# Two graph layers and two top-2 mixtures of experts: the choice of experts made panel by panel inside the convolutions, gates carried in the gathered rows, w3 resident instead of w1, second products two blocks behind

## The chip, the cores and the metric

The kernel runs on one core of a Trainium2 chip. TensorE (PE) multiplies, VectorE (DVE), ScalarE (ACT) and GpSimd (POOL) work element by element, and SyncE (SP) only issues transfers. Each engine takes its own instructions strictly in order and waits on semaphores for the others. The metric is the device time in microseconds of one execution, as the median over runs.

## The reference

There are N = 3125 nodes with 256 features (D) and 50000 edges (src, dst). Four residual blocks follow each other, each on the layernorm of x:

```python
def sage(x, W_l, b_l, W_r):                       # mean over incoming edges
    return (segment_sum(x[src], dst) / max(deg, 1)) @ W_l + b_l + x @ W_r

# block 1: two SAGE convolutions and a product
h = relu(sage(ln(x), W1_l, b1, W1_r)); h = relu(sage(h, W2_l, b2, W2_r))
x = x + h @ W3 + b3
# block 2: 16 experts of width 512, the best two of each node
p = softmax(ln(x) @ gate_w + gate_b); top2, renormalised to sum 1
x = x + sum_e gate_e * ((silu(ln(x) @ w1[e]) * (ln(x) @ w2[e])) @ w3[e])
# block 3: on ln(x): three GCN convolutions of the first 64 features (relu),
#          a dynamic convolution weighted by gelu(x @ W1 + b1) @ W2 + b2,
#          joined with the other 192 features
x = x + x_full @ W_aggr + b_aggr
# block 4: 8 experts of width 512, the best two, without gates
x = x + sum_e mask_e * (gelu(ln(x) @ W1[e] + b1[e]) @ W2[e] + b2[e])
```

## The kernel before

Nodes are held in NT = 25 tiles of 128 rows, grouped in panels of 512 (TPP = 4 tiles): six full ones and one of a single tile. A dense matrix of edge counts is built once in fp8 (`at8`) and both graph layers multiply with it. The program is written in the order of the computation. A framework assigns the tiles to memory pools, sets the semaphores, and orders each engine's instructions ahead of the run by their place in the program and by modelled times; at run time each engine keeps that order. A tile with `bufs=k` may have k instances alive, and a new one waits until the oldest is no longer read.

**Convolutions of layer 0.** `sage` walks the panels. For each, `panel_of` casts 25 blocks of `at8` into `blk` tiles (128x512), five alive at once. `cast` shares them out by their number over ACT and DVE, and over POOL too in the second graph (where `three` is set and seven tiles are alive). PE multiplies each block into `pa` (line 576), the sums are copied to `agg` (582), and then every tile gets its products and its `done` function. For conv2 this is `convolution2`: when a panel is done, it stores x to `xb0`, normalises into `rows` (lines 384 to 390; the square root is ACT's), stores these to `xnd0` by SP, transposes each tile and writes its scores into the kept tile `scores0` (516).

**Choice of experts.** It starts when all panels are done, behind an If (line 718) whose body is for graphs that cannot take the fast way. `resident` loads the whole of w1 (16 loads of 512 KB, line 865) on ACT's queue. Then softmax over all 25 tiles at once (lines 970 to 975), `top2` (400 elements per operation), and `route`: PE forms the running counts of each expert in f32, and every chosen pair of node and expert gets a position in a list sorted by expert, in blocks of 128 rows. To invert that list, `route` runs a loop over two choices of 25 tiles each: DVE makes a one-hot `row` (835) and a two-part `what` (837, 845) of node number and gate, and PE multiplies them (848). The result is `idx`, the node of every row of every block, and `gate` (855, 857).

**Experts.** `experts` walks the blocks, 64 in layer 0 and 56 in layer 1. `begin` issues the block's streamed weights on SP and the gather of its rows on POOL (897), two blocks ahead. `hidden` transposes the rows (`pt`, `xT`), multiplies with the first weights (`ph`, 918) and forms `hid`. `finish`, one block behind, transposes `hid`, multiplies with the last weight (`pe`, 937 and 942), scales with the gate into `y` (944), and POOL adds `y` to `xb` by an indirect DMA (945). In layer 0 w1 is resident and w2 and w3 are streamed, 1 MB per block; in layer 1 both weights are resident, and a broadcast bias of 256 KB is streamed.

**Second graph.** The rows are read back and normalised. Three GCN passes walk the panels (`pc`, line 1096), and with the first two go the dynamic convolution's panels. In the last pass `finish` makes the output rows of a panel: products, the residual sum, normalisation, transposes and scores into `scores1`. Then `resident` loads both weights of layer 1 on ACT's queue, and `top2`, `route` and `experts` run again.

Of the kernel before, what the change touches and what calls it, by code (L numbers as in the profile page):

```python
# [8 lines left out]
F32 = mybir.dt.float32  # L9
# [9 lines left out]
P = 128  # L19
N = 3125  # L20
# [32 lines left out]
def kernel(ctx: ExitStack, tc: tile.TileContext, a, out: bass.AP):  # L53
# [20 lines left out]
    def open_rows(c):  # L74
        here["rows"] = c.enter_context(tc.tile_pool(name="rows", bufs=2))
# [40 lines left out]
    scores0 = keep.tile([P, NT, NE0], F32, name="scores0")  # L116
    scores1 = keep.tile([P, NT, NE1], F32, name="scores1")
# [4 lines left out]
    xnd0, xnd1, xb0, xb1 = (dram.tile([NR, D], F32, name=n) for n in ("xnd0", "xnd1", "xb0", "xb1"))  # L122
# [10 lines left out]
    def build_sorted(c):  # L133
# [4 lines left out]
        sums = scores1.rearrange("p t e -> p (t e)")[:, : 2 * NG]  # L138
        gl = c.enter_context(tc.tile_pool(name="sl", bufs=1))
        gk = c.enter_context(tc.tile_pool(name="sk", bufs=2))  # L140
        gw = c.enter_context(tc.tile_pool(name="sw", bufs=3))
# [41 lines left out]
        def prepare():  # L183
            for i, (c0, w) in enumerate(PANELS):
# [41 lines left out]
                ohr = gk.tile([P, P, WN], F16, name="ohr", bufs=1)  # L226
# [24 lines left out]
        def count():  # L251
# [3 lines left out]
            for g in range(NG):  # L255
                w0 = g * GW
                ohk = gw.tile([P, 2, NF, 4], F16, name="ohk")
                onehot(ohk, io_key, keys[:, w0 : w0 + GW], 2)
                ohl = gw.tile([P, 2, P, 4], F16, name="ohl")
# [177 lines left out]
    def panel_of(exact, loads, c0, w, three=False):  # L437

        if not exact:
            for k in range(NT):  # L440
                blk = loads.tile([P, PW], F32R, name="blk", bufs=7 if three else 5)
                cast(k, blk[:, :w], at8[c0 // PW][:, k, :], three)
                yield k, blk[:, :w]
            return
# [38 lines left out]
    def top2(s, n, small):  # L483

        def first_max(v, i):
            m = small.tile([P, NT], F32, name=f"m{i}")
            nc.vector.tensor_reduce(m, v, AX.X, OP.max)
            hit = small.tile([P, NT, n], F32, name=f"hit{i}")  # L490
            nc.vector.tensor_tensor(hit, v, m[:, :, None].to_broadcast([P, NT, n]), OP.is_equal)
            nc.vector.scalar_tensor_tensor(
                hit, hit, -float(P), iota[:, None, :n].to_broadcast([P, NT, n]), op0=OP.mult, op1=OP.add
            )
            at_ = small.tile([P, NT], F32, name=f"at{i}")
            nc.vector.tensor_reduce(at_, hit, AX.X, OP.min)
            nc.vector.tensor_scalar(at_, at_, float(P), None, op0=OP.add)
            oh = small.tile([P, NT, n], F32, name=f"oh{i}")
            nc.vector.tensor_tensor(
                oh,  # L500
                iota[:, None, :n].to_broadcast([P, NT, n]),
                at_[:, :, None].to_broadcast([P, NT, n]),
                OP.is_equal,
            )
            return m, oh

        m1, oh1 = first_max(s, 1)
        rest = small.tile([P, NT, n], F32, name="rest")
        nc.vector.scalar_tensor_tensor(rest, oh1, -3e38, s, op0=OP.mult, op1=OP.add)
        m2, oh2 = first_max(rest, 2)  # L510
        return m1, oh1, m2, oh2

    def scores(s, xT, t, w, bias, n):
        pg = ps_one("pg", [P, n])
        product(pg, xT, w)
        nc.vector.tensor_add(s[:, t, :], pg, bias)


    class First:


        def __init__(self, c):
            self.pool = lambda name, bufs: c.enter_context(tc.tile_pool(name=name, bufs=bufs))
            self.rows = self.pool("rows0", NT + 1)
# [10 lines left out]
        def weights2(self, c):  # L535
            cw = c.enter_context(tc.tile_pool(name="cw2", bufs=1))
# [88 lines left out]
    def convolution2(f, exact, loads):  # L625
# [15 lines left out]
        for panel in sage(f, exact, loads, parts, f.w2l, f.b2, own[1], done2):  # L641
# [7 lines left out]
            nc.sync.dma_start(rows_in(xnd0, c0, w), rows[:, :n, :])  # L649
            for i in range(n):  # L650
                xT = f.n.tile([P, KD, P], F32, name="xT")
                transpose_tile(xT, rows[:, i, :])
                scores(scores0, xT, c0 // P + i, f.gw, f.gb, NE0)
# [8 lines left out]
    with ExitStack() as c:  # L662
# [45 lines left out]
        open_psum(ctx, 2)  # L708
        with ExitStack() as c1:
            open_rows(c1)  # L710
            behind = rows_tile()[:, 0, :]
            nc.vector.memset(behind, 0.0)
            for t in (xnd0, xnd1, xb0, xb1):
                nc.scalar.dma_start(t[NP:, :], behind)
# [492 lines left out]
```

## Time and profile before

| what | time |
|---|---|
| runs of the kernel | 1933.12 us median (1928.09 to 1934.69) |
| profiled execution | 1928.86 us, span 1927.1 us, clock 0.916 |
| end of conv2's scores to first expert transpose, layer 0 | 623.58 to 711.48 |
| experts of layer 0 | 712 to 1112 |
| second graph's passes | 1166 to 1560 |
| last scores to first expert transpose, layer 1 | 1560.17 to 1611.10 |
| experts of layer 1 | 1611 to 1909 |

Times are microseconds from the start of the span. The page's slices cut the span in 40 parts of about 48 us, and a digit is the busy share of an engine in tenths; PEclk is the granted clock of TensorE in the same scale. In a table of windows each row has the window, its sum, and per engine the busy time with the number of instructions. A row of the timeline gives start and duration, engine, line, the operation with its output and inputs, and in brackets how long the engine had been idle and what released it. A group row gives the busy time, the mean of one instruction in nanoseconds, and the idle time in front of the group. Names are the program's: `xg` are gathered rows, `xb` the rows to which results are added, `w_all` a resident weight.

### The profile page before, as it was taken

What the parts mean: (1) busy time and instruction counts of PE and PEld (TensorE: products, weight loads), DVE (VectorE), ACT (ScalarE), POOL (GpSimd) and SP (SyncE); (2) the same over time, 40 slices, a digit from 0 to 9 for tenths busy, and PEclk for the clock granted to TensorE, in tenths of its full rate; (3) what the DMA queues carried; (4) which work ended last, traced back from release to release, by engine and by line L of the source; (5) the groups of instructions that cost most, each with busy time, mean ns of one, the idle gap of its engine ahead of it and who ended that gap; (6) DMA issues with size and microseconds to landing.
All of it is one profiled execution on the core that took longest, in us unless ns stands there. A gap on an engine that the chain in (4) does not pass through costs nothing. (4 is left out here: it accounts for less than half of the span.)

```text
span 1927.1 us, 23952 instructions
## 1 busy us (share of the span) xinstructions
PE 1671.2 (87%) x7696; PEld 1159.7 (60%) x7696; DVE 879.0 (46%) x2298; ACT 660.8 (34%) x1574; POOL 492.2 (26%) x513
## 2 busy tenths in 40 slices
PE   5899999799997189999999937879889758999995
PEld 3777777677776055555555525546567545556553
DVE  5866664244542562222222266547547464333231
ACT  3766665233331002222222226437446101222221
POOL 4411110100000013444434334204213002544542
PEclk9999999899997559999999958999989757999998
DMA  3311111711210426777777630000002162444444
GB/s 115 104 53 47 47 48 36 243 45 44 66 48 29 175 93 193 216 217 213 212 211 213 174 96 18 1 1 1 1 8 92 58 218 54 104 102 99 101 102 103
DMA packets 145977, 192.81 MB, mean 100 GB/s; under 512 B 11728, under 2 KB 105279, under 8 KB 145775
## 3 DMA queue, kind: packets, MB, share of 16 engines
q1 hardware_dynamic: 106108, 137.28, 22.2%
q0 software_dynamic: 23936, 33.83, 9.7%
q10 hardware_dynamic: 15794, 20.01, 3.1%
q8 instruction: 68, 1.11, 0.2%
q14 instruction: 71, 0.57, 0.1%
HBM read 148.61 MB, written 45.67 MB: 101 GB/s over the span
## 5 line engine op out<-in xcount | busy, mean ns | idle before, releaser
L576 PE MATMUL pa<-blk,hl 128*128 128x512 f32 (+1 forms) x1400 | 366.0, 401 | 1.8 <-ACT blk L431 1.8
L897 POOL DMA_INDIRECT xg<-xnd,idx x120 | 118.1, 984 | 670.5 <-DVE gate L857 330.6
L576 PEld LDWEIGHTS pa<-blk,hl 128*128 128x128 f32 x1400 | 249.0, 196 | 43.5 <-ACT blk L431 2.3
L431 ACT CAST blk<-at 128x512 fp32r<-128x512 fp8e4 (+1 forms) x378 | 209.5, 572 | 125.7 <-PE pa L576 64.9
L918 PE MATMUL ph<-w_all,xT 128*128 x480 | 240.8, 625 | 9.5 <-ACT xT L399 0.4
L945 POOL DMA_INDIRECT xb<-y,idx x120 | 190.7, 1589 | 164.5 <-DMA xb<-y,idx 87.3
L433 DVE CAST blk<-at 128x512 fp32r<-128x512 fp8e4 (+1 forms) x392 | 171.7, 456 | 99.7 <-PE pa L576 75.9
L399 ACT COPY xT<-pt 128x256 f32<-128x256 f32 x195 | 72.6, 372 | 319.6 <-PE pt L398 317.8
L1096 PE MATMUL pc<-blk,g 128*128 128x512 f32 (+1 forms) x525 | 144.5, 411 | 16.3 <-ACT blk L431 12.9
L989 DVE TENSOR_TENSOR hid<-hid,ph 128x512 f32<-128x512 f32 x64 | 44.0, 687 | 239.7 <-ACT hid L988 239.7
L918 PEld LDWEIGHTS ph<-w_all,xT 128*128 128x128 f32 x480 | 80.4, 190 | 99.3 <-issue 62.2
L435 POOL CAST blk<-at 128x512 fp32r<-128x512 fp8e4 (+1 forms) x105 | 71.7, 689 | 256.6 <-PE pc L1096 172.9
L1096 PEld LDWEIGHTS pc<-blk,g 128*128 128x128 f32 x525 | 94.3, 200 | 49.4 <-issue 14.6
L937 PE MATMUL pe<-w,hTs 128*128 128x256 f32 x512 | 121.3, 379 | 1.0 <-ACT hTs L933 1.0
L937 PEld LDWEIGHTS pe<-w,hTs 128*128 128x128 f32 x512 | 97.0, 190 | 41.1 <-issue 29.7
L918 PE MATMUL ph<-w,xT 128*128 128x512 f32 x256 | 120.4, 592 | 0.0
L268 ACT ACTIVATE at<-pcount 128x400 fp8e4<-128x400 f32 x196 | 97.4, 502 | 49.4 <-PE pcount L264 48.2
L944 DVE TENSOR_SCALAR y<-pe,gate 128x256 f32<-128x256 f32 x120 | 58.1, 484 | 122.7 <-PE pe L942 94.1
L988 ACT ACTIVATE hid<-ph 128x512 f32<-128x512 f32 x64 | 38.2, 597 | 217.9 <-PE ph L918 217.9
L937 PE MATMUL pe<-w_all,hTs 128*128 x448 | 106.0, 379 | 1.8 <-ACT hTs L933 1.8
L937 PEld LDWEIGHTS pe<-w_all,hTs 128*128 128x128 f32 x448 | 85.0, 190 | 36.8 <-issue 25.8
L264 PE MATMUL pcount<-ohk,ohl 128*128 128x100 f16 x784 | 93.7, 271 | 3.0 <-ACT at L268 1.5
(251 smaller groups left out, 2358.1 us busy)
## 6 DMA issues: line engine op xcount, KB each, us to landing
w<-in_L_ffn_w_dram SPq DMA_DIRECT2D x128, 512.0 KB, 5.4
bin<-in_L_ffn_b_dram SPq DMA_DIRECT2D x56, 256.0 KB, 3.6
w_all<-in_L_ffn_w_dram ACTq DMA_DIRECT2D x16, 512.0 KB, 10.2
w_all<-in_L_ffn_W_dram ACTq DMA_DIRECT2D x16, 512.0 KB, 9.9
h1d<-hl SPq DMA_DIRECT2D x25, 256.0 KB, 2.0
hl<-h1d SPq DMA_DIRECT2D x25, 256.0 KB, 4.9
xp<-in_x_dram SPq DMA_DIRECT2D x12, 512.0 KB, 4.7
mine<-own SPq DMA_DIRECT2D x12, 512.0 KB, 3.9
```

The costliest lines, as they stand in the source:

```text
L264: nc.tensor.matmul(pw[:, w * NF : (w + 1) * NF], ohl[:, b, :, w], ohk[:, b, :, w], start=True, stop=True)
L268: nc.scalar.activation(at8[o // PW][:, :, o % PW : o % PW + 4 * WN].rearrange("p k (w r) -> p w k r", r=WN), pw[:, : 4 * NF].rearrange("p ...
L399: nc.scalar.copy(dst, pt)
L431: nc.scalar.copy(dst, src)
L433: nc.vector.tensor_copy(dst, src)
L435: nc.gpsimd.tensor_copy(dst, src)
L576: nc.tensor.matmul(pa[:, m, :w], parts[k][:, i, m * P : (m + 1) * P].bitcast(one), blk, start=(k == 0 and i == 0), stop=(k == NT - 1 and i ...
L897: nc.gpsimd.indirect_dma_start(out=xg, out_offset=None, in_=xnd[:, :], in_offset=bass.IndirectOffsetOnAxis(ap=idx[:, b : b + 1], axis=0),)
L918: ran.append(nc.tensor.matmul(ph[:, i, :], xT[:, k, :], weight_of(b, weights, i, k), start=(k == 0), stop=(k == KD - 1)))
L937: nc.tensor.matmul(po, hT[:, j, :], weight_of(b, weights, n_in, j), start=(j == 0), stop=(j == n_hid - 1 and b_out is None))
L945: nc.gpsimd.indirect_dma_start(out=xb[:, :], out_offset=bass.IndirectOffsetOnAxis(ap=idx[:, b : b + 1], axis=0), in_=y, in_offset=None, co ...
L1096: nc.tensor.matmul(pc[:, :w], g[:, k].rearrange("p i q -> p (i q)").bitcast(one), blk, start=(k == 0), stop=False,)
```

## The change

- A class `Router` takes the place of `top2` and of the first half of `route`. Its `panel` is called by conv2, and by `finish` of the second graph, once the scores of a panel stand. It makes the softmax (layer 0 only), the two best experts, gates, counts and ranks of the panel, with two f16 products on PE, and the one-hot rows of its tiles in f16, which stay in the kept tile `onehots`.
- Its `route` does what needs the totals: the first block of each expert, then for each of the two choices one comparison over all blocks and tiles at once, one product on DVE, one copy on ACT and 25 f16 products on PE.
- The gates of layer 0 and the numbers of their experts are written as four more columns of `xnd0`, one transfer per panel on SP. A gather brings them with the row, and `finish` picks the gate that belongs to the block's expert.
- w3 is the resident weight of layer 0, and w1 and w2 are streamed. The loads of `resident` go by POOL's queue instead of ACT's, in both layers.
- In layer 0 the second products run two blocks behind the first instead of one. `hid` gets three tiles, `xg` five; `y` has two instead of three in both layers.
- To make room: `blk` five tiles everywhere instead of seven in the second graph, `rows0` 25 tiles instead of 26, single instances of `rows`, `g`, `ew` and `nT` in the second graph, normalisation in place there. The constants are made before conv2.

The core of the diff (what is not shown: the build of the graph using `onehots` as scratch space, the way for other graphs, the constants):

```diff
-                blk = loads.tile([P, PW], F32R, name="blk", bufs=7 if three else 5)
+                blk = loads.tile([P, PW], F32R, name="blk", bufs=5)
...
+    class Router:
+        ohs_ = keep.tile([P, 2, NT, NE0], F16, name="ohs")
+        high = keep.tile([P, 2, NT], F32, name="high")
+        before_ = keep.tile([P, NT + 1, NE0], F16, name="before")
...
+        def panel(self, small, c0, s, gates=None):
...
+            if gates is not None:
+                red = tile_("red", [P, n])
+                nc.vector.tensor_reduce(red, s, AX.X, OP.max)
+                nc.vector.tensor_sub(s, s, wide(red))
+                nc.scalar.activation(s, s, AF.Exp)
+                nc.vector.tensor_reduce(red, s, AX.X, OP.add)
+                nc.vector.reciprocal(red, red)
+                nc.vector.tensor_mul(s, s, wide(red))
+            best, at_ = tile_("best", two), tile_("at", two)
+            v = s
+            for c in range(2):
+                nc.vector.tensor_reduce(best[:, c, :], v, AX.X, OP.max)
+                hit = tile_("hit")
+                nc.vector.tensor_tensor(hit, v, wide(best[:, c, :]), OP.is_equal)
+                nc.vector.scalar_tensor_tensor(
+                    hit, hit, -float(P), iota[:, None, :n_exp].to_broadcast(shape), op0=OP.mult, op1=OP.add
+                )
+                nc.vector.tensor_reduce(at_[:, c, :], hit, AX.X, OP.min)
+                nc.vector.tensor_scalar(at_[:, c, :], at_[:, c, :], float(P), None, op0=OP.add)
+                oh = self.ohs[:, c, t0 : t0 + n, :]
+                nc.vector.tensor_tensor(oh, iota[:, None, :n_exp].to_broadcast(shape), wide(at_[:, c, :]), OP.is_equal)
+                if c == 0:
+                    v = tile_("rest")
+                    nc.vector.scalar_tensor_tensor(v, oh, -3e38, s, op0=OP.mult, op1=OP.add)
+            if gates is not None:
+                nc.vector.tensor_add(red, best[:, 0, :], best[:, 1, :])
+                nc.vector.reciprocal(red, red)
+                for c in range(2):
+                    nc.vector.tensor_mul(gates[:, :n, c], best[:, c, :], red)
+                    nc.vector.tensor_copy(gates[:, :n, 2 + c], at_[:, c, :])
...
+            both = tile_("both", dtype=F16)
+            nc.vector.tensor_add(both, chosen[:, 0], chosen[:, 1])
+            for i in range(n):
+                nc.vector.tensor_add(self.before[:, t0 + i + 1, :], self.before[:, t0 + i, :], both[:, i, :])
+            pr = ps_one("ranks", shape)
+            nc.tensor.matmul(pr, tri16, both, start=True, stop=False)
+            nc.tensor.matmul(pr, ones16, self.before[:, t0 : t0 + n, :], start=False, stop=True)
+            of = tile_("of", four)
+            for c in range(2):
+                nc.vector.tensor_tensor(of[:, c], chosen[:, c], pr, OP.mult)
+            rank = tile_("rank", two)
+            nc.vector.tensor_reduce(rank, of, AX.X, OP.add)
+            ranki, low = tile_("ranki", two, I32), tile_("low", two, I32)
+            nc.vector.tensor_copy(ranki, rank)
+            nc.vector.tensor_single_scalar(low, ranki, P - 1, op=OP.bitwise_and)
+            nc.vector.tensor_single_scalar(ranki, ranki, 7, op=OP.arith_shift_right)
+            low16 = tile_("low16", two, F16)
+            nc.vector.tensor_copy(low16, low)
+            nc.vector.tensor_copy(self.high[:, :, t0 : t0 + n], ranki)
...
+            for c in range(2):
+                nc.vector.tensor_tensor(
+                    self.rows[:, c, t0 : t0 + n, :], iota16[:, None, :].to_broadcast([P, n, P]),
+                    low16[:, c, :, None].to_broadcast([P, n, P]), OP.is_equal,
+                )
+        def route(self, small):
...
+            past = tile_("past", [P, nb, n_exp])
...
+            for c in range(2):
+                of = tile_("of", [P, NT, n_exp], F16)
+                nc.vector.tensor_tensor(of, self.ohs[:, c], first[:, None, :].to_broadcast([P, NT, n_exp]), OP.mult)
+                blk = tile_("blk", [P, NT])
+                nc.vector.tensor_reduce(blk, of, AX.X, OP.add)
+                blk16 = tile_(f"blk16_{c}", [P, NT], F16)
+                nc.vector.tensor_add(blk16, blk, self.high[:, c, :])
+                is_ = tile_(f"is_{c}", [P, nb, NT], F16)
+                shape = [P, nb, NT]
+                nc.vector.tensor_tensor(
+                    is_, iota16[:, :nb, None].to_broadcast(shape), blk16[:, None, :].to_broadcast(shape), OP.is_equal
+                )
+                what = tile_(f"what{c}", [P, 2, nb, NT], F16)
+                nc.scalar.activation(what[:, 1], is_, AF.Copy, scale=pcol)
+                nc.vector.tensor_tensor(what[:, 0], is_, tiles16[:, None, :].to_broadcast(shape), OP.mult)
+                for t in range(NT):
+                    nc.tensor.matmul(
+                        pi.rearrange("p a b -> p (a b)"), self.rows[:, c, t, :], what[:, :, :, t].rearrange("p a b -> p (a b)"),
+                        start=(c == 0 and t == 0), stop=(c == 1 and t == NT - 1),
+                    )
...
-            self.rows = self.pool("rows0", NT + 1)
+            self.rows = self.pool("rows0", NT)
...
-                scores(scores0, xT, c0 // P + i, f.gw, f.gb, NE0)
+                scores(s[:, i, :], xT, f.gw, f.gb, NE0)
+            gates = f.small.tile([P, TPP, 4], F32, name="gates", bufs=2)
+            router0.panel(f.small, c0, s, gates)
+            nc.sync.dma_start(rows_in(xnd0[:, D:], c0, w), gates[:, :n, :])
...
-            nc.scalar.dma_start(t[:, e], w[e].rearrange("(k p) n -> p k n", p=P))
+            nc.gpsimd.dma_start(t[:, e], w[e].rearrange("(k p) n -> p k n", p=P))
...
-            xg = hids.tile([P, D], F32, name="xg", bufs=4)
+            xg = hids.tile([P, wide], F32, name="xg", bufs=3 + depth)
...
-            hid = hids.tile([P, n_hid * P], F32, name="hid")
+            hid = hids.tile([P, n_hid * P], F32, name="hid", bufs=depth + 1)
...
-            y = hids.tile([P, D], F32, name="y", bufs=3)
-            nc.vector.tensor_scalar(y, po, gate[:, b : b + 1], None, op0=OP.mult)
+            y = hids.tile([P, D], F32, name="y", bufs=2)
+            if gated is None:
+                nc.vector.tensor_copy(y, po)
+            else:
+                each = hids.tile([P, 2], F32, name="each")
+                gate = hids.tile([P, 1], F32, name="gate")
+                nc.vector.scalar_tensor_tensor(
+                    each, xg[:, D + 2 :], gated[:, b : b + 1], xg[:, D : D + 2], op0=OP.is_equal, op1=OP.mult,
+                    accum_out=gate,
+                )
+                nc.vector.tensor_scalar(y, po, gate, None, op0=OP.mult)
...
-            hid = hidden(b, weights, bi, xg)
-            if last is not None:
-                finish(*last)
-            last = (b, hid, weights)
+            open_.append((b, hidden(b, weights, bi, xg), weights, xg))
+            if len(open_) > depth:
+                finish(*open_.pop(0))
...
-    w1_all = resident(ffn0.enter_context(tc.tile_pool(name="res0", bufs=1)), "w1_all", a["L0_ffn_w1"])
+    w3_all = resident(ffn0.enter_context(tc.tile_pool(name="res0", bufs=1)), "w3_all", a["L0_ffn_w3"])
...
-            [a["L0_ffn_w1"], a["L0_ffn_w2"]], None, a["L0_ffn_w3"], silu_gate, stay=[w1_all],
+            [a["L0_ffn_w1"], a["L0_ffn_w2"]], None, a["L0_ffn_w3"], silu_gate, gated=exp, stay=[None, None, w3_all], depth=2,
...
-        open_rows(c)
+        open_rows(c, 1)
...
-            x = xp.tile([P, TPP, D], F32, name="x")
-            nc.sync.dma_start(x[:, :n, :], rows_in(xb0, c0, w))
-            rows = rows_tile()
-            normalize(rows, x, n)
+            rows = xp.tile([P, TPP, D], F32, name="x")
+            nc.sync.dma_start(rows[:, :n, :], rows_in(xb0, c0, w))
+            normalize(rows, rows, n)
...
-                        scores(scores1, nT, t0 + i, gw1, gb1, NE1)
+                        scores(s[:, i, :], nT, gw1, gb1, NE1)
+                    router1.panel(small, c0, s)
```

## The prediction

> **What bounds the kernel now.** I read the engine totals and the slices first, then the busy time by stage, then the timeline of the two places where TensorE stands still.
>
> ```profile
> PE 1671.2 (87%) x7696; PEld 1159.7 (60%) x7696; DVE 879.0 (46%) x2298; ACT 660.8 (34%) x1574; POOL 492.2 (26%) x513
> ...
> PE   5899999799997189999999937879889758999995
> ...
> DVE  5866664244542562222222266547547464333231
> ...
> PEclk9999999899997559999999958999989757999998
> ```
>
> PE is busy 87 % of the span. Its row is near 9 everywhere except at the start and in two holes, slices 13 and 14 and slice 33; there PEclk falls to 0.5. The holes are the choice of experts of layer 0 and of layer 1. The stages, with busy time per engine:
>
> ```profile
> core 0: us, PE busy (x) PEld busy (x) DVE busy (x) ACT busy (x) POOL busy (x), PEclk, DMA share, GB/s
> 475.00:509.00 34.00, 34.00 (x163) 26.56 (x163) 16.27 (x47) 12.27 (x26) 0.00 (x0) 1.00 0.20 62
> 628.00:655.00 27.00, 0.02 (x1) 0.05 (x1) 10.34 (x25) 1.82 (x2) 0.00 (x0) 0.50 0.87 311
> 655.00:671.00 16.00, 2.98 (x4) 1.12 (x4) 13.10 (x49) 0.00 (x0) 0.00 (x0) 0.50 0.00 1
> 671.00:705.00 34.00, 32.42 (x100) 25.05 (x100) 33.07 (x159) 0.00 (x0) 0.00 (x0) 0.50 0.00 0
> 712.00:1112.00 400.00, 391.60 (x1407) 234.55 (x1406) 102.02 (x192) 88.29 (x194) 159.37 (x123) 0.99 0.72 206
> 1430.00:1500.00 70.00, 67.25 (x343) 51.68 (x341) 53.81 (x153) 43.55 (x88) 20.39 (x30) 1.00 0.22 70
> 1576.00:1607.00 31.00, 28.96 (x100) 25.04 (x100) 30.10 (x164) 0.00 (x0) 0.00 (x0) 0.50 0.34 109
> 1611.00:1909.00 298.00, 290.04 (x1120) 174.79 (x1120) 89.60 (x168) 77.97 (x169) 140.20 (x109) 0.99 0.46 96
> ```
>
> 475–509 is one panel of conv2: PE never idles, DVE is busy 16.3 of 34.0 us. 628–705 is the choice of experts of layer 0: 27 us in which w1 streams in and almost nothing computes, 16 us of DVE alone, 34 us in which DVE builds one-hot rows (33.1 busy) and PE multiplies them at clock 0.50. 712–1112 and 1611–1909 are the experts, PE-bound at 97–98 %. 1430–1500 is the last pass of the second graph with its output rows: PE 96 %, but DVE 77 % too. 1576–1607 is the one-hot loop of layer 1. Now the first hole in order of time:
>
> ```profile
> 623.58 0.17 DVE L516 TENSOR_TENSOR scores<-pg,row_L_ffn_gate_b 128x16 f32<-128x16 f32 x1 [2.33 <-PE pg L410]
> 627.59 15.53 ACTq L865 DMA_DIRECT2D w_all<-in_L_ffn_w_dram  x16
> 628.01 0.57 DVE L970 TENSOR_REDUCE red<-scores 128x25 f32<-128x400 f32 x1 [4.26 <-PEq L718]
> ...
> 643.16 1.28 ACT L972 ACT_TABLE_LOAD   x1 [20.71 <-DMA w_all<-in_L_ffn_w_dram]
> 644.45 0.54 ACT L972 ACTIVATE scores<-scores 128x400 f32<-128x400 f32 x1
> ...
> 704.75 0.22 DVE L855 SCALAR_TENSOR_TENSOR idx<-none,rows 128x64 int32<-128x64 f32 x1
> ...
> 705.86 0.98 POOL L897 DMA_INDIRECT xg<-xnd,idx  x1 [330.57 <-DVE gate L857]
> ...
> 711.48 0.66 PE L398 MATMUL pt<-ident,xg 128*128 128x128 f32 x2 [7.09 <-DMA xg<-xnd,idx]
> ```
>
> The last scores stand at 623.58, the first expert transpose at 711.48: 87.9 us. Three things fill it: PE's branch behind the If (DVE waits 4.26 us for it); Exp, held 20.7 us behind the issue of w_all on ACT's queue; and DVE's chain up to idx at 704.75. From idx to the first transpose are 6.7 us. Layer 1, read the same way, has its last scores at 1560.17, idx at 1606.88 and the first transpose at 1611.10: 50.9 us.
>
> ```profile
> L897 POOL DMA_INDIRECT xg<-xnd,idx x120 | 118.1, 984 | 670.5 <-DVE gate L857 330.6
> ...
> L945 POOL DMA_INDIRECT xb<-y,idx x120 | 190.7, 1589 | 164.5 <-DMA xb<-y,idx 87.3
> ...
> L516 DVE TENSOR_TENSOR scores<-pg,row_L_ffn_gate_b 128x16 f32<-128x16 f32 x4 | 0.7, 175 | 3.0 <-PE pg L410 3.0
> ```
>
> These price what POOL does per DMA (a gather of 128 rows 0.98 us, a scatter-add 1.59) and a small DVE operation (0.175 us; dependent ones start 0.20 apart).
>
> **The change part by part.** The profiled execution took 1928.86 us (span 1927.1), 0.2 % under the median of the three runs, 1933.12. The sum is made against 1928.86 and about 4 us are added at the end.
>
> *Panel work in conv2.* For a panel of four tiles the new router issues 37 small DVE operations (softmax 5, top-2 13, gates 6, counts 5, ranks 8) and two one-hot rows of 128x512. At 0.20 us, and 0.6 us for a row (casts of that shape take 0.42, an f32 copy 0.69), that is 7.4 + 1.2 = 8.6 us. DVE goes from 16.3 to about 25 of 34.7 us per panel and stays below PE. But the 37 run as a burst, and DVE also makes half of the five-deep `blk` tiles, which PE eats at 34.7/25 = 1.4 us each: five cover 7 us, so each burst can cost PE up to 2 us; the two f16 rank matmuls cost PE under 0.5 us. Cost: 6 panels × 1 us = +6 (0 to +25). The gates' DMA on SP waits for the burst; behind it stand the next panel's loads of `mine`, 22 us ahead of use by the trace, so I charge nothing; without that cover it would be some 2 us per panel. Exp among Sqrts makes ACT switch tables twice per panel. The row: load 1.28 us at 643.16, its activation follows at 644.45, no drain to be seen. The Trainium skill, "ScalarE: Activation LUTs", section "Table sets: the hidden batching unit", says to batch by set, and "What ACT_TABLE_LOAD costs" prices a switch at 1.28 + 1.38 us of drain. That speaks against this change: 14 switches are 18 us of ACT by the row and 37 by the page. ACT is busy 12 of 34 us, so both hide; only the last panel's switch is on the path, 1.3 or 2.7 us. I use the row.
>
> *Choice, layer 0.* On the path after the last scores: about 30 small operations of the last, one-tile panel up to the rank matmul, with the table switch, 6 us; PE's branch, 4.3 us as now, over the rest of the panel. Then `route`: totals and counts 1.7, ends 1.4, past and its reduce 2.8 (1024 elements; L802's and L809's 1.2 us each), then per choice 0.6 + 0.6 + three 1600-element operations at 1.1 ≈ 4.6, the second's matmuls (25 × 0.21 at half clock) 5.2, idx 0.9: 21 us. So idx comes 31 us after the scores instead of 81, and PE could start at 38. The w1 wait of Exp is gone. What is late next is w3: its 16 loads now stand on POOL's queue ahead of the gathers. Memory for w3 comes free only where w1's did, so they start with `route`. Their data, 8.4 MB at 311 GB/s, is 27 us, so the first gather cannot land before about 41. Their issue is not in the trace: w1's sixteen took ACT 15.5 us; a POOL DMA costs at least a gather's 0.98, at most 3.9 if it goes by rows (512 of 1 KB against 128). I take 2 us, a little over the scatter's row, as both handle few rows: 10.3 + 32 + 5.6 from gather to transpose = 48 us, −40. With 1 us it is −46, with 3.9 us (78 us) −10. A second rule against it: "SBUF — State Buffer", section "Who interferes with whom", says that POOL cannot write descriptors while DVE runs a two-port operation. The trace's gathers take 0.94 to 1.03 us whether DVE works or not, so I keep 2; by the page the loads stretch with `route`'s DVE copies and the high end is nearer.
>
> *Experts, layer 0.* The stream is 1 MB a block as before (w1 and w2 for w2 and w3), PE's work is the same: period 6.16 us. Two small DVE operations for the gate add 0.2 us where DVE is a quarter busy: nothing; without that cover 64 × 0.2 = 13 us. Second products two blocks behind leave PE's order nearly as it is; at best they close the 0.26 us per block in which PE waits for xT, 64 × 0.26 = −16. At the end one more scatter is serialised: +2. With `y` at two buffers the scatter chain has 5 us of room here and 2 in layer 1, whose period is 5.22: +1 (0 to +5).
>
> *Second graph.* Normalising in place and single buffers before the passes: +2 (0 to +5). `blk` goes from 7 to 5 buffers: my estimate is 0.35 us on each of about 14 panel passes, +5 (0 to +8). In the last pass the router adds 26 small operations and two rows, 26 × 0.19 + 1.0 = 6 us per panel, to a stage where DVE is busy 0.77 of 18.8 = 14.5 us: 20.5 us, above the period. DVE becomes the bound; with its waits I take 21.1, +2.3 × 6 = +14 (+5 to +25).
>
> *Choice, layer 1.* Last panel 5.6 us, `route` 17.5, gather 4.2: 27.4 for 50.9, −23.5. Its weights move to POOL too, but POOL has no casts after about 1510 and the memory is free by then; hidden. If they start only at 1559, as w1_all did, 16 × 2 us end 8 us behind the new idx at 1583, and 16 × 3.9 us end 38 behind it.
>
> Sum: +6 −40 +2 +1 +2 +5 +14 −23.5 = −33.5, so 1895.4, and 1899 on the median's side.
>
> **The rivals.** *POOL's issue takes the gain.* At 3.9 us per load layer 0 gains 10 in place of 40: sum −3.5, 1929 with the 4 us of the median, and past 1940 if layer 1's loads are late as well. For: 1 KB rows, software descriptors, gathers in the same queue. Against: gathers and scatters show a cost per instruction of 1.0 to 1.6 us.
>
> *The panel work stalls PE (slower).* One mechanism: the burst stands ahead of the casts in DVE's order, and the rank matmul stands ahead of the next products in PE's. If PE stands for a whole burst, 12 full panels lose 8.6 or 6 us each, 88 us in place of the 20 charged: −33.5 + 68 = +34, 1967. It decides from (33.5 + 5.8)/12 = 3.3 us of stall per panel above my charge. For: DVE at 77 % in the last pass, in-order engines, one pool of one buffer. Against: in conv2 DVE is half idle and PE runs on cast tiles that ACT makes too.
>
> *More gain.* POOL issues at 1 us (−46), bursts interleave with casts (0), the last pass pays only 5, the 0.26 us gaps close by half (−8): about −63, 1870. For: half of DVE is free in conv2. Against: the last pass has no such room.
>
> **How the numbers follow.** 0.3 % (5.8 us) is about what a measurement of this kernel can tell from no change. My forecast has 0.50, all of it faster; more gain 0.20; POOL's issue 0.15 (0.04 faster, 0.08 within, 0.03 slower); panel stalls 0.15 (0.04 faster where they stay small, 0.11 slower). Faster 0.50 + 0.20 + 0.04 + 0.04 = 0.78; same 0.08; slower 0.03 + 0.11 = 0.14. The range reaches from a little past the more-gain case, 1866, to the edge of slower, 1938, and so leaves out about 0.14 above and a few hundredths below. The forecast's own range is 1880 to 1920.
>
> **What would show it.** Right: first transpose about 48 us after the last scores of layer 0 (27 in layer 1), conv2 panels at 35.7 us (34.7 now), last pass at about 21 us per panel with DVE over 90 % busy, block periods 6.16 and 5.22 unchanged, loads of w3 about 2 us apart on POOL. Wrong: loads 4 us apart with the first gather after them (first rival); PE idle over 3 us per panel behind ranks or `blk` (second); a block period over 6.2, which would mean that scatters, `y` or the longer gathered rows bound the experts.

## The result and the profile after

The changed kernel takes 1920.24 us (median; 1916.64 to 1921.38) against 1933.18: ratio 0.9933, interval 0.9917 to 0.9948, a gain of 13 us where 34 were forecast. The direction was right, the size was not. Its profiled execution took 1919.90 us (span 1918.1, against 1927.1 before). First lines of the changed kernel's page: the engines' totals, PE's slices, the granted clock, and the group of w3's loads on POOL.

```profile
PE 1652.2 (86%) x7618; PEld 1127.4 (59%) x7618; DVE 893.1 (47%) x2509; ACT 682.5 (36%) x1596; POOL 509.8 (27%) x543
...
PE   4899999799998399999999459789797647999995
...
PEclk9999999999998599999999769999998657999998
...
L906 POOL DMA_DIRECT2D w_all<-in_L_ffn_w_dram x16 | 12.1, 767 | 268.2 <-PE totals L604 263.6
```

The hole of layer 0 has shrunk: slices 13 to 15 read 8, 3 and 9 where they read 7, 1 and 8. The hole of layer 1 has grown forwards: slices 31 to 33 read 7, 6 and 4 where they read 9, 7 and 5, and the clock falls with them, well ahead of the choice of experts, in the last pass of the second graph. The loads on POOL cost 0.77 us each. The stages, in windows of the changed kernel:

```profile
core 0: us, PE busy (x) PEld busy (x) DVE busy (x) ACT busy (x) POOL busy (x), PEclk, DMA share, GB/s
479.00:514.00 35.00, 34.97 (x167) 26.92 (x166) 22.77 (x86) 15.29 (x29) 0.00 (x0) 1.00 0.21 61
631.00:641.00 10.00, 0.22 (x2) 0.13 (x2) 5.72 (x40) 0.37 (x2) 0.00 (x0) 0.50 0.04 8
641.00:664.00 23.00, 11.51 (x51) 6.31 (x51) 12.64 (x31) 3.26 (x2) 12.05 (x16) 0.50 0.88 294
664.00:671.00 7.00, 0.00 (x0) 0.00 (x0) 0.18 (x1) 0.00 (x0) 4.72 (x5) 0.50 1.03 353
671.00:1071.00 400.00, 392.45 (x1407) 235.95 (x1408) 116.22 (x319) 88.11 (x194) 157.17 (x123) 0.99 0.76 208
1425.00:1500.00 75.00, 59.80 (x267) 42.41 (x265) 55.85 (x203) 29.74 (x64) 13.58 (x23) 0.86 0.17 53
1573.00:1600.00 27.00, 10.36 (x53) 6.42 (x52) 13.67 (x56) 2.92 (x2) 2.98 (x3) 0.50 0.08 21
```

A conv2 panel (479–514) has 22.8 us of DVE in 35 where it had 16.3 in 34, and PE still never idles. The choice of layer 0 (631–671) is short. The experts are as before. The row to stop at is 1425–1500: in the kernel before, PE was busy 67.3 of 70 us here at clock 1.00; now it is 59.8 of 75 at 0.86. Yet DVE, at 55.9 of 75, is no busier than it was.

Both traces cut at the same events give the account of the 9 us between the spans:

| stage | before | after | change | forecast |
|---|---|---|---|---|
| start to first scores of conv2 | 425.8 | 429.6 | +3.8 | 0 |
| conv2, first to last scores | 197.8 | 201.4 | +3.6 | +6 |
| last scores to first expert transpose, layer 0 | 87.9 | 40.2 | −47.7 | −40 |
| from there to the first read of the added rows | 405.6 | 408.1 | +2.5 | +2 |
| from there to pwT of the last pass's first panel | 316.3 | 325.5 | +9.2 | +7 |
| from there to the last scores of layer 1 | 126.8 | 167.6 | +40.8 | +14 |
| last scores to first expert transpose, layer 1 | 50.9 | 30.3 | −20.6 | −23.5 |
| from there to the end | 316.0 | 315.4 | −0.6 | +1 |

The first line need not be the change's: in the kernels below whose code up to there is the same, the first scores stand anywhere from 425.0 to 430.0. One line carries most of the miss, the last pass. The choice of layer 0 in the changed kernel, in order of time:

```profile
630.98 0.17 DVE L489 TENSOR_TENSOR s<-pg,row_L_ffn_gate_b 128x16 f32<-128x16 f32 x1 [2.33 <-PE pg L413]
...
641.55 0.17 PE L604 MATMUL totals<-before,ones__3915 128*128 128x16 f16 x1 [5.71 <-DVEq L885]
...
650.33 1.63 ACT L649 ACTIVATE what<-is,pcol 128x1600 f16<-128x1600 f16 x1 [18.51 <-DVE is L645]
...
652.01 11.34 PE L652 MATMUL nodes<-what,onehots 128*128 128x128 f16 x50 [10.29 <-ACT what L649]
...
663.96 0.22 DVE L661 SCALAR_TENSOR_TENSOR idx<-node,nodes 128x64 int32<-128x64 f32 x1
...
665.07 1.04 POOL L940 DMA_INDIRECT xg<-xnd,idx  x1 [6.19 <-DVE idx L661]
...
671.14 0.66 PE L401 MATMUL pt<-ident,xg 128*128 128x128 f32 x2 [7.80 <-DMA xg<-xnd,idx]
```

The last scores stand at 630.98, PE's next work after the If at 641.55 (10.6 us; 10.3 forecast), idx at 663.96, the first transpose at 671.14. POOL has finished w3's loads before idx is there, so the first gather starts 1.1 us behind idx: the issue of the loads, which I took for the longest of the three paths, is not on it.

Now the last pass. First what PE waited for in 1405–1565 (us in all, number of waits, the longest), then PE's rows and DVE's rows around one panel's end:

```profile
PE ranks L568 <- DVE both L564: 18.1, 6, 4.0
```

```profile
1464.90 3.62 PE L413 MATMUL po<-w_L_gnn_W_aggr,xT 128*128 128x256 f32 x16
...
1476.70 0.82 PE L413 MATMUL pg<-w_L_ffn_Wg,nT 128*128 128x8 f32 x4 [0.52 <-ACT nT L402]
1481.48 0.21 PE L568 MATMUL ranks<-both,tri 128*128 128x32 f16 x1 [3.96 <-DVE both L564]
1481.62 1.97 PE L1167 MATMUL pwT<-gT,ws 128*64 128x512 f32 x2
1483.52 0.21 PE L569 MATMUL ranks<-before,ones__3915 128*128 128x32 f16 x1
1483.66 1.97 PE L1172 MATMUL pi<-ident,dinv 128*64 128x128 f32 x8
...
1489.15 6.08 PE L413 MATMUL po<-w_L_gnn_W_aggr,xT 128*128 128x256 f32 x16
```

```profile
1477.56 0.17 DVE L489 TENSOR_TENSOR s<-pg,row_L_ffn_bg 128x8 f32<-128x8 f32 x1 [1.44 <-PE pg L413]
...
1481.25 0.17 DVE L564 TENSOR_TENSOR both<-ohs 128x32 f16<-128x32 f16 x1
```

PE makes the last scores of a panel by 1477.52 and then stands for 3.96 us. The next instruction in its order is the rank product, and that needs `both`, the end of a chain of 15 DVE operations from `s` on (1477.56 to 1481.42). Behind it stand pwT and pi, which need nothing from that chain, and all that follows from them, the next `po` included. From one `po` to the next are 23 to 28 us where they were 18 to 20. Of the six waits five are 3.2 to 4.0 us long; in the first panel PE waits only 0.2 us, because `pc` products of a later panel stand in front of the rank product and fill the time. The whole pass, from the first pwT to the last scores, in the kernel before and in the changed one:

```profile
1433.41:1560.17 126.76, 105.91 (x482) 80.29 (x481) 72.75 (x219) 50.91 (x110) 19.50 (x29) 0.83 0.23 70
```

```profile
1404.79:1572.37 167.58, 121.15 (x494) 85.69 (x494) 104.57 (x389) 52.17 (x111) 29.91 (x45) 0.75 0.31 103
```

DVE is busy 31.8 us more than before, but only 62 % of the longer pass. PE stands 46.4 us where it stood 20.9.

### The profile page after: what moved, and what is told of

The parts are those of the page before. It is cut to its first block, busy times and chain, and to the rows that moved or that the text cites. A ratio compares the mean times of both kernels' runs of the same rounds, so it can differ in the third digit from the quotient of the medians.

```text
span 1918.1 us, 24044 instructions
## 1 busy us (share of the span) xinstructions
PE 1652.2 (86%) x7618; PEld 1127.4 (59%) x7618; DVE 893.1 (47%) x2509; ACT 682.5 (36%) x1596; POOL 509.8 (27%) x543
## 5 line engine op out<-in xcount | busy, mean ns | idle before, releaser
L961 PE MATMUL ph<-w,xT 128*128 128x512 f32 x512 | 238.8, 610 | 5.6 <-ACT xT L402 0.8
L980 PE MATMUL pe<-w_all,hTs 128*128 x960 | 227.2, 379 | 3.0 <-ACT hTs L976 3.0
L980 PEld LDWEIGHTS pe<-w_all,hTs 128*128 128x128 f32 x960 | 182.1, 190 | 78.1 <-issue 55.5
L1136 PE MATMUL pc<-blk,g 128*128 128x512 f32 (+1 forms) x525 | 150.2, 420 | 23.9 <-ACT blk L434 13.7
L961 PEld LDWEIGHTS ph<-w,xT 128*128 128x128 f32 x512 | 92.6, 191 | 114.4 <-issue 88.3
L961 PE MATMUL ph<-w_all,xT 128*128 x224 | 112.0, 624 | 4.2
L267 PE MATMUL pcount<-onehots 128*128 128x100 f16 x784 | 93.8, 270 | 3.0 <-ACT at L271 1.5
L267 PEld LDWEIGHTS <-onehots 128*128 128x128 f16 x784 | 68.8, 118 | 28.3 <-issue 12.8
L906 POOL DMA_DIRECT2D w_all<-in_L_ffn_w_dram x16 | 12.1, 767 | 268.2 <-PE totals L604 263.6
L1209 ACT ACTIVATE hid<-hid 128x512 f32<-128x512 f32 x56 | 35.3, 630 | 133.8 <-DVE hid L1208 133.8
```

Source lines behind the costliest of these rows:

```text
L267: nc.tensor.matmul(pw[:, w * NF : (w + 1) * NF], ohl[:, b, :, w], ohk[:, b, :, w], start=True, stop=True)
L961: ran.append(nc.tensor.matmul(ph[:, i, :], xT[:, k, :], weight_of(b, weights, i, k), start=(k == 0), stop=(k == KD - 1)))
L980: nc.tensor.matmul(po, hT[:, j, :], weight_of(b, weights, n_in, j), start=(j == 0), stop=(j == n_hid - 1 and b_out is None))
L1136: nc.tensor.matmul(pc[:, :w], g[:, k].rearrange("p i q -> p (i q)").bitcast(one), blk, start=(k == 0), stop=False,)
```

## The experiments

Each ratio is against the kernel before on the same chip; the change's own is 0.9933 (0.9917 to 0.9948). Theory A: PE stands in its own order behind the rank products. Rival B, which was my forecast's mechanism: DVE has more work than the pass has time.

**Ranks one panel later.** Same work; the rank products and all that follows them in the panel's chain are issued after the next panel's pwT and pi.

```diff
+            return lambda: self.ranks(small, n, t0, both, chosen)
+
+        def ranks(self, small, n, t0, both, chosen):
...
             pr = ps_one("ranks", shape)
...
-                    router1.panel(small, c0, s)
...
+                    pending.append(router1.panel(small, c0, s))
...
+                            if pending:
+                                pending.pop()()
                             finish(c0, w)
...
+                pending.pop()()
```

> The changed kernel, with one edit: in the second graph the two rank products on PE and all that follows them in the panel's chain are issued one panel later, behind the next panel's pwT and pi. DVE has the same work. Theory A (PE, in order, stands behind the rank product until DVE's chain has delivered): the 18.1 us in which ranks waits for both disappear, the clock stays up to the fifth panel, the last pass falls from about 27 us per panel to about 21, and the time to 1890 to 1902. Rival B (DVE is the bound of the last pass, whatever PE's order): PE waits as long in other places, the last pass stays at 25 to 27 us per panel, the time at 1913 to 1921.

Measured: 1889.43 us, ratio 0.9787 (0.9767 to 0.9807), just under theory A's range and far from B's. Four of the rank products in PE's order:

```profile
1448.74 0.19 PE L578 MATMUL ranks<-both,tri 128*128 128x32 f16 x1
...
1491.48 0.19 PE L578 MATMUL ranks<-both,tri 128*128 128x32 f16 x1 [1.33 <-DVE both L564]
...
1514.26 0.19 PE L578 MATMUL ranks<-both,tri 128*128 128x32 f16 x1 [2.73 <-DVE both L564]
...
1534.91 0.21 PE L578 MATMUL ranks<-both,tri 128*128 128x32 f16 x1 [3.05 <-DVE both L564]
```

In the first panels PE no longer waits for them; at the end, where no pc products are left to stand in between, it still waits 1 to 3 us. The pass (first pwT to last scores) takes 141.2 us: 167.6 with the change, 126.8 before. Its row, and what PE waits for in it that it hardly waited for before:

```profile
1401.66:1542.85 141.19, 110.74 (x494) 79.99 (x494) 96.39 (x389) 52.18 (x111) 31.94 (x45) 0.84 0.37 122
```

```profile
PE pc L1146 <- DVE blk L436: 8.2, 7, 2.0
...
PE ranks L578 <- DVE both L564: 7.1, 3, 3.0
```

Of the 40.8 us, 26.4 came from the order: PE has the same 494 products and DVE the same 389 operations. The edit also moves the end of DVE's chain (ranks and one-hot rows) one panel later, and the run does not separate that from the move on PE; what shrinks in the trace are PE's waits at the rank products (18.1 to 7.1 us) and at `po` for its input xT, which stands behind them (7.0 to 0.6 us), while PE's wait for DVE's casts grows (1.8 to 8.2). In all PE stands 16.0 us less, and its products take 10.4 us less, at a mean clock of 0.84 instead of 0.75. What is left of the loss, 14.4 us, is by chance the size that I had given to the whole: DVE is busy 68 % of the pass and is not its bound, and the two waits shown, 8.2 and 7.1 us, stand where the kernel before had 0.3 and none. About 3 of the 14.4, as a run below shows, is there without any panel work. The rest of the 31 us between the two kernels is mostly the start (425.0 against 429.6), which is not this edit's.

**Filling PE's wait.** In the changed kernel the granted clock is lower where PE stands more: 1.00 in 1425–1450 with PE 89 % busy, 0.66 in 1475–1500 with 72 %. To see whether that is the loss, 24 products of 128x128 into one unused tile (`keep_warm`) are put in front of each rank product.

```diff
+            if keep_warm is not None:
+                keep_warm()
             pr = ps_one("ranks", shape)
```

> The changed kernel, with 24 idle products of 128x128 (0.14 us each at full clock, 3.4 us) put on PE in front of each panel's rank product in the second graph; their result is not used. They only fill the wait. Theory A1 (part of the loss is the lower clock that follows PE's standing still: po took 6.1 and 6.7 us in panels 4 and 5 where it took 3.7 before): the clock stays near 1.00 through the last pass and the time falls by 8 to 15 us, to 1905 to 1912. Rival (the clock is only a sign, the chain through DVE sets the pace): the clock rises, but the time stays at 1918 to 1924.

Measured: 1923.98 us, ratio 0.9961 (0.9945 to 0.9977): no gain, rather 0.3 % more than the change. PE's rows of one panel, and of the fifth:

```profile
1448.19 2.87 PE L1115 MATMUL warm<-identr,xc 128*128 128x128 f32 x24
1452.52 0.19 PE L572 MATMUL ranks<-both,tri 128*128 128x32 f16 x1 [1.46 <-DVE both L566]
...
1537.64 0.18 PE L572 MATMUL ranks<-both,tri 128*128 128x32 f16 x1 [8.61 <-DVE both L566]
```

The clock stays between 0.86 and 0.93 from 1425 to 1500 (1.00, 0.93 and 0.66 in the same thirds with the change), and from one `po` to the next are still 24 to 26 us; over the first four panels 5 of the 29 us are won that the change loses there. So in these panels the lower clock is the smaller part of the loss. In the last three the clock is hardly above the change's (0.70, 0.50 and 0.57 from 1500 to 1573, against 0.59, 0.53 and 0.54), and the run says nothing of its part there. The fifth panel lost more than was won, for another reason. What DVE waited for in 1405–1575:

```profile
DVE x L1128 <- DMA x<-xb: 10.2, 1, 10.2
```

DVE stands 10.2 us for the last panel's load of x. There are two x tiles, so this load goes out when an earlier panel's x is stored. That store, issued at 1515.3, stands among the loads of layer 1's weights, which start on POOL at 1510; the load of x follows at 1527.9, and DVE goes on at 1536.0. This makes the run a poor measure of the total; what it says of the clock rests on the four panels before.

**Panel work of layer 1 undone.** One call for 25 tiles behind the second graph; the cut buffers stay cut.

```diff
-                    router1.panel(small, c0, s)
...
+        router1.panel(small, 0, all_scores(NE1))
+        idx, exp, expi = router1.route(small)
```

> The changed kernel, with the panel work of layer 1 undone: scores of all tiles are kept, and the panel's code runs once for 25 tiles behind the second graph. Everything else is as changed, the five blk buffers and single instances included. Theory A and B alike (the panel work costs the last pass its 41 us): the pass goes back to about 146 us, and about 21 us of DVE (26 operations at 0.3, 25 counts at 0.18, 50 one-hot tiles at 0.17) come on the path behind the scores: time 1900. Rival C (the cut buffers cost the last pass): the pass stays at 187 us and the time rises to about 1940.

Measured: 1891.67 us, ratio 0.9795 (0.9776 to 0.9814). The pass goes back to 129.8 us (the 146 and 187 us of the expectation count it from some 19 us earlier), the way from last scores to first transpose grows from 30.3 to 43.4. All but 3 us of the 40.8 belonged to the panel work. And done at once it costs 13.1 us: making it panel by panel in this pass, in this order, was a loss of 37.8 − 13.1 = 25 us. The cut buffers, rival C, are no more than the 3 us.

**Panel work of layer 0 undone**, in the same way.

> The changed kernel, with the panel work of layer 0 undone in the same way: one panel call for 25 tiles behind conv2, one transfer of gates. If the panel work is what conv2 pays, conv2 gives back about 3.6 us, while 37 operations at 0.4, 25 counts and 50 one-hot tiles, about 28 us, come on the path, and the gathers wait some 3 us for the gates: time 1940 to 1948. If the work were as well done at the end, the time would stay within 3 us of 1920.

Measured: 1933.73 us, ratio 1.0006 (0.9995 to 1.0016). The gain of the change is gone, though less than I expected was lost: conv2 gives back 1.9 us, and the way from scores to transpose grows from 40.2 to 57.9. In conv2 the panel work pays, 18 us for 2: there the changed kernel's trace shows only 1.0 us of wait at the rank products in six panels.

**Depth and resident weight.** The second products one block behind (`depth=1`), and w1 resident again with the same depth.

> The changed kernel, with the second products of layer 0 one block behind instead of two (three hid tiles become two, five xg four). Theory (PE's order was already tight, PE 97 % busy): the block period stays within 0.05 us of the changed kernel's, the tail is about 2 us shorter, the time 1917 to 1922. Rival (two blocks behind saves the 0.26 us per block in which PE waited for xT, while something else in the experts gave the same amount back): the period rises by 0.1 to 0.26 us, the time to 1927 to 1937.

> The changed kernel, with w1 resident instead of w3 and the second products one block behind, as before the change; loads on POOL's queue, panel work and gates as changed. Theory (w_all's data has landed before the first gathered rows do, so it does not matter which weight it is): the first expert transpose and the time stay within 3 us, 1917 to 1923. Rival (w3 is worth its place because the first products would have to wait for w1's data): PE's first ph waits for w_all by 5 to 15 us, time 1925 to 1935.

Measured: 1915.47 us, ratio 0.9923 (0.9909 to 0.9938), and 1917.76 us, ratio 0.9933 (0.9916 to 0.995). Neither can be told from the change's 0.9933. Block periods, from `y` to `y` over 31 or 32 blocks, are 6.16 (before), 6.17 (change), 6.16 (one behind), 6.17 (w1 resident). These two parts of the change neither gain nor cost anything that the runs can tell.

**The queue of the resident weights.** On top of late ranks (the ranks one panel later), the loads go back to ACT's queue.

```diff
-            nc.gpsimd.dma_start(t[:, e], w[e].rearrange("(k p) n -> p k n", p=P))
+            nc.scalar.dma_start(t[:, e], w[e].rearrange("(k p) n -> p k n", p=P))
```

> The kernel with the ranks one panel later (1889.4), with the resident weights' loads on ACT's queue as before the change. Theory (ACT, in order, is held by the issue as in the kernel before, 15.5 us): in layer 0 the issue runs from about 640 to 655 and the first copy of what, due at 650, waits 5 us; in layer 1 it waits 0 to 3 us, while the early loads no longer meet the last pass's load of x (2.2 us of wait): time 1892 to 1898. Rival (POOL's queue brings nothing): 1887 to 1891.

Measured: 1907.69 us, ratio 0.9884 (0.9867 to 0.9902), 18 us more; both of my expectations fell. The choice of layer 0 in this kernel:

```profile
637.80 19.46 ACTq L916 DMA_DIRECT2D w_all<-in_L_ffn_w_dram  x16
...
657.44 3.15 ACT L659 ACTIVATE what<-is,pcol 128x1600 f16<-128x1600 f16 x2 [29.23 <-DMA w_all<-in_L_ffn_w_dram]
659.11 11.34 PE L662 MATMUL nodes<-what,onehots 128*128 128x128 f16 x50 [21.23 <-DMA w_all<-in_L_ffn_w_dram]
...
671.07 0.22 DVE L671 SCALAR_TENSOR_TENSOR idx<-node,nodes 128x64 int32<-128x64 f32 x1
```

The issue holds ACT for 19.5 us, not 15.5. ACT's half of `what` for choice 0 starts at 657.44, 11 us behind DVE's half of the same tile (646.31), and idx comes at 671.07: from last scores to first transpose are 49.8 us where late ranks had 40.2. Layer 1 goes the same way (issue 1552 to 1571, `what` at 1571.5; 36.8 us instead of 29.6), which I had priced at 0 to 3 us. On SP's queue instead:

> The kernel with the ranks one panel later (1889.4), with the resident weights' loads on SP's queue. It tells whether POOL's queue matters or only that it is not ACT's, which cost 18 us. Theory (any queue will do whose engine has nothing due): 1886 to 1890, since 2.2 us of wait for x go too. Rival (only POOL is free early enough): 1892 to 1900.

Measured: 1891.37 us, ratio 0.9807 (0.9787 to 0.9826), between my two forecasts and not to be told from POOL's. What matters here is not POOL but that the queue's engine has nothing due: with late ranks the move off ACT is worth about 18 us.

**The buffers of blk.** Seven tiles again, with layer 1's panel work at the end (room: ew, nT and ws in the idle `onehots`), and four tiles, with late ranks.

> The kernel with layer 1's panel work behind the second graph (1891.7), with seven blk tiles in the second graph again; the room for them comes from putting ew, nT and ws into the kept tile onehots, which is idle there. Theory (the cut from seven to five sets the pace of the passes: a panel of the first passes takes 8.54 us in the changed kernel and took 7.95 before): the period goes back to 7.95, 12 panels give 7 us, the time 1882 to 1886. Rival (the period rose for another reason[...]): it stays at 8.5 and the time at 1889 to 1894.

> The kernel with the ranks one panel later (1889.4), with four blk tiles instead of five in the second graph. Theory of blk: each tile less costs at least as much as one of the two that were cut (0.3 us per panel of the first passes), so the period goes from 8.54 to 8.9 or more and the time to 1896 to 1910. Rival (blk is deep enough at five): period 8.5, time 1887 to 1892.

Measured: 1887.56 us, ratio 0.978 (0.9766 to 0.9794), and 1906.46 us, ratio 0.9885 (0.987 to 0.99). Two neighbouring panels' `pw` in the first pass, in the kernel before (seven), the change (five), with seven again, and with four:

```profile
1186.06 1.00 PE L1111 MATMUL pw<-ws,gT 128*128 128x64 f32 x8
...
1194.01 1.00 PE L1111 MATMUL pw<-ws,gT 128*128 128x64 f32 x8
```

```profile
1151.38 1.00 PE L1151 MATMUL pw<-ws,gT 128*128 128x64 f32 x8
...
1159.95 1.00 PE L1151 MATMUL pw<-ws,gT 128*128 128x64 f32 x8
```

```profile
1145.70 1.00 PE L1152 MATMUL pw<-onehots,gT 128*128 128x64 f32 x8
...
1153.65 1.00 PE L1152 MATMUL pw<-onehots,gT 128*128 128x64 f32 x8
```

```profile
1149.47 1.00 PE L1161 MATMUL pw<-ws,gT 128*128 128x64 f32 x8
...
1159.13 1.00 PE L1161 MATMUL pw<-ws,gT 128*128 128x64 f32 x8
```

The period is 7.95, 8.57, 7.95 and 9.66 us, and the other panels of the two passes agree: five tiles set the pace, and seven undo it. Cutting them costs 0.6 us per panel of the first two passes, where the run with seven is 5.4 us shorter than the same kernel with five. The whole was 4 us shorter (1887.56 against 1891.67, with intervals that overlap), not 7, and the last pass gave 1.7 us back. What DVE waited for in 1400–1550 with seven tiles again:

```profile
DVE x L1118 <- DMA x<-xb: 8.7, 1, 8.7
```

**Two that brought nothing.** With seven tiles and the loads on SP's queue, to take that wait away:

> The kernel with layer 1's panel work at the end and seven blk tiles (1887.6), with the resident weights' loads on SP's queue. In that kernel the loads of layer 1 start on POOL at about 1490, beside the last pass's load of x, for which DVE then waits 8.7 us. On SP they stand behind that load and behind the last stores. Theory (the early loads delay x): the wait goes, the sixth panel of the last pass takes 20 us instead of 24.6, time 1879 to 1884. Rival (the loads, now later, are missing at the start of the experts, or SP's issue delays the first weights): what is won is given back, time 1886 to 1895.

Measured: 1887.86 us, ratio 0.9783 (0.9761 to 0.9805), the same. The wait is gone from the trace, but from the fifth `po` to the sixth are still 23.3 us instead of 24.6: the clock now falls one panel earlier (`po` of the fifth takes 6.3 us, not 3.7). Why it falls there, no run shows. And late ranks with the last nine tiles at the end:

> The kernel with the ranks one panel later, and the panel work of the last nine tiles of layer 1 done in one call behind the second graph: in the kernel with late ranks PE still waits 1.3, 2.7 and 3.1 us for them in the fifth to seventh panels, where no pc products are left to fill in. Theory A (these waits are on the path): the last scores come 7 to 9 us earlier and the nine-tile call costs 10 us in place of the last tile's 5.6: time 1884 to 1889. Rival (DVE has as much to do and nothing is saved): 1889 to 1894.

Measured: 1893.47 us, ratio 0.9811 (0.9793 to 0.9829). The pass is 3.7 us shorter than with late ranks alone, the way to the first transpose 4.1 us longer; the rival's number held.

The best versions are late ranks, and the panel work of layer 1 at the end with seven `blk` tiles: both are 2.1 to 2.2 % under the kernel before, some 1.5 % under the change, and the runs do not tell them apart.

## Why the prediction was wrong

*Panel work in conv2*: right in kind, 3.6 us for a forecast of 6. DVE's burst hides; as an estimate from the trace, twelve rank products of 0.2 us and 1.0 us of wait at them make 3.4. The last panel's table switch was not even on the path: it ran from 629.88 for 1.28 us, beside the last scores (630.98), and Exp started at 631.60, 0.03 us after its input. The 1.38 us of drain that the Trainium skill's "ScalarE: Activation LUTs", section "What ACT_TABLE_LOAD costs", adds to a switch does not show here either: ACT was idle for 0.45 us behind the load, until DVE's input was there.

*Choice, layer 0*: −47.7 for −40. The step that failed is POOL's price, 2 us per load: a load took 0.77, and the last six started 1.5 us apart. That is below the low end that I had set from the gather's 0.98. No stretching by DVE's copies showed: the loads took 0.75 to 0.77 us each while DVE was busy 12.6 of the 23 us (641–664). With the low price my own sum gave −46.

*Experts*: right, +2.5 for +2; depth and resident weight are worth nothing, as argued.

*Passes before the last*: right in total (+9.2 for +7), but `blk` costs 0.6 us per panel, not 0.35.

*Last pass*: this is the wrong step. I wrote "DVE becomes the bound", and took +2.3 us per panel from DVE's busy time. DVE did not become the bound: of the over 90 % that I named as the sign, 62 % came. The measured loss was 40.8 us, and the run with late ranks splits it: 14.4 remain with the same work, and 26.4 come from the order in which it is issued, above all from the place of two products of 0.2 us in PE's queue. I counted the added work on the engine that does it. For PE I charged the products themselves in conv2 (under 0.5 us), and in this pass nothing. I did not ask what stands behind them in PE's queue while they wait. The rival "panel work stalls PE" named the mechanism, and put its deciding point at 3.3 us above the charge per panel; over twelve panels it would have made the kernel slower. It came true in six panels of the twelve: 26.4/6 = 4.4 us above the charge in each on average, none in conv2. My argument against it, that conv2's PE runs on cast tiles, held for conv2 alone, where I had looked.

*Choice, layer 1*: −20.6 for −23.5; the gathers took 7.4 us from idx to the first transpose instead of 4.2. Why, no run shows.

The sum with the measured terms: +3.6 −47.7 +2.5 +9.2 +40.8 −20.6 −0.6 = −12.8, and with the start's +3.8 the 9 us between the spans. That −12.8 is also the difference of the medians is chance: it leaves out the start.

## What to carry to other kernels

When work is moved from a serial stage into a busy one, count not only its operations against the free time of their engine, but find every small instruction that it puts on the *bottleneck's* queue, and ask what that one waits for and what stands behind it. A product of 0.2 us that waits for a chain of 15 operations can cost the chain; issued one panel later, with other products in between, it was no longer waited for. And the same move can pay in one stage and lose in another: 18 us won for 2 in conv2, 25 us lost in the last pass.

## What was not expected of the hardware

Sixteen loads of 512 KB, issued on POOL's queue, took 0.75 to 0.8 us each; after the first nine or ten they started 1.4 to 1.5 us apart, and the trace shows each of them waiting for the transfer of an earlier one; on ACT's queue the same sixteen held the engine 19.5 us. Early loads are not free either: the last pass's store and load of x stood among those of the weights, and DVE waited 6.8 to 10.2 us for x in three kernels; with the loads later, on SP's queue, this wait was gone, without a gain in time. And the granted clock was only 0.53 to 0.59 in three windows where PE still shows 49 to 65 % busy (1500 to 1573 in the changed kernel); beside a wait of 4 us per panel `po` took 6.1 us instead of 3.6. In the kernel before the clock fell as well, but only at the end of the pass (0.57 in the sixth panel; 0.63 in the fourth with the change).
